# A feed-forward by pairs of tiles with seven products for eight, and weight sums made by the first tokens

## The chip, the cores and the metric

The kernel runs on one core of a Trainium2 chip. The metric is the time of one execution on the device, in microseconds (us); the time before is the median of three runs. Engines have short names: PE is TensorE's products, PEld its weight loads, DVE is VectorE, ACT is ScalarE, POOL is GpSimd, SP is the queue that issues all DMAs here.

## The reference

Two transformer layers over 32 sequences of 64 tokens, 512 wide, all in fp32. With `ln` for a layer norm:

```python
x = x + xattn0(ln(x), ctx)      # layer 0: one head, softmax over the 64 context rows
x = x + ffn0(ln(x))             # layer 0: a sparse feed-forward
x = x + xattn1(ln(x), ctx)      # layer 1: 32 query heads, 8 key/value heads of 128
x = x + ffn1(ln(x))             # layer 1: one dense product under two masks

def ffn0(xf):                               # 2048 tokens
    inter = xf @ c1_w.T @ c2_w.T            # rank 16, then 1792
    blk = inter.reshape(-1, 56, 32)
    idx = argmax(blk, -1) + arange(0, 1792, 32)   # the first of equals
    h = relu(einsum("bkm,bm->bk", w1[idx], xf))   # one of each 32 rows of w1
    return einsum("bk,bkm->bm", h, w2t[idx])
```

## The kernel before

The 2048 tokens are 16 tiles of 128 (`X[t]`), kept on chip throughout. Stages follow each other: attention of layer 0 by pairs of tiles, its feed-forward, attention of layer 1 in 32 units (four groups `T` of 512 tokens, eight groups `g` of heads), the last feed-forward. The kernel is written in program order against tiles taken from pools; a scheduler puts each engine's instructions in a fixed order at build time by simulated readiness, earlier code first, and adds the waits. On the chip each queue runs in that order. A pool that takes the bytes of released pools waits for all of their users.

**Feed-forward of layer 0.** `prep(t)` normalises a tile, turns it (`pt`, L181), copies it to `xT` and makes `z`, its 16 coefficients (`pz`, L404). `front(xT, z, half)` handles two quarters of 448 columns: `pi` (L414) is `z` against `C2`, sixteen rows deep; `ph` (L419) is `xT` against `W1` in four chunks, with all 1792 columns computed and the unchosen ones zeroed. The argmax is L421 (block maximum), L423 (equal to it), L426 on POOL (times 32..1, so that the first of equals wins), L427 (maximum), L428 (equal). L431 makes `g = max(ph, 0) * e`. `back(t, half, g)` turns `g` in seven pieces (`ptg`, L444), copies them to `gT` (L445) and multiplies by `W2` (`po`, L449); L454 adds to `x`. `finish` turns the first four tiles for layer 1.

**Large products of layer 1.** `winograd` makes a product of two by two quarters with seven products instead of eight. It needs four sums of the quarters on either side (`four_sums`, L99 to L107, on POOL) and adds into three banks of PSUM; `keep` takes a bank's value midway, `put` takes a finished quarter:

```python
mm(1, b1, True);  e1 = keep(0, b1)
mm(5, b2, True);  e5 = keep(1, b2)
mm(6, b1, False); u2 = keep(2, b1)
mm(2, b3, True);  put(0, 0, b3, e1)
mm(7, b1, False); put(1, 1, b1, e5)
mm(3, b2, False); put(0, 1, b2, u2)
mm(4, b1, False); put(1, 0, b1, None)
```

**Weight sums.** The sums of layer 1's weights (8 groups of `wq`, 8 of `wo`, 4 pairs of `wkv`) are made once, while layer 0 runs: `sum_weights` is called 8 times in the attention and 32 times in the feed-forward, and each call makes the sums of quarters `r` loaded by the call before (POOL), stores them to DRAM (L171, SP) and loads the next four (L176, SP). `load_weights` then loads, for each unit of layer 1, the quarters and sums that its seven products need (L505).

**A unit of layer 1** is `project_kv` (each second unit), `project_q`, `norms`, `keys`, `softmax` (L646, L653 to L663, three of its operations on POOL), `project_out` of the unit before (`wo`, L707), `attend` (`pta`, `pv` at L683) and `out_sums`.

Of the kernel before, what the change touches and what calls it, by code (L numbers as in the profile page):

```python
# [11 lines left out]
ALU = mybir.AluOpType  # L12
# [22 lines left out]
def tile_kernel(  # L35
# [39 lines left out]

    XG = [xpool.tile([P, 4, D], F32, name=f"x_{i}", tag=f"x_{i}") for i in range(4)]
# [19 lines left out]
    def four_sums(eng, s, w11, w12, w21, w22, right):  # L96

        if right:
            eng.tensor_tensor(s[0], w12, w11, ALU.subtract)  # L99
            eng.tensor_tensor(s[1], w22, s[0], ALU.subtract)  # L100
            eng.tensor_tensor(s[2], w22, w12, ALU.subtract)
            eng.tensor_tensor(s[3], w21, s[1], ALU.subtract)
        else:
            eng.tensor_tensor(s[0], w21, w22, ALU.add)
            eng.tensor_tensor(s[1], s[0], w11, ALU.subtract)  # L105
            eng.tensor_tensor(s[2], w11, w21, ALU.subtract)
            eng.tensor_tensor(s[3], w12, s[1], ALU.subtract)  # L107
# [3 lines left out]
    ORDER = (1, 5, 6, 2, 7, 3, 4)  # L111
    LEFT = {1: 0, 2: 1, 3: 7, 4: 3, 5: 4, 6: 5, 7: 6}
# [43 lines left out]
    to_sum = []  # L156
    for g in range(G):
        if g % 2 == 0:
            to_sum.append((kv_quarter, g // 2, WKS, True))
        to_sum.append((q_quarter, g, WQS, False))  # L160
        to_sum.append((o_quarter, g, WOS, True))
    loaded = []

    def sum_weights():

        if loaded:
            n, sums, right, r = loaded.pop()
            s = [wprep.tile([P, 2, 256], F32, name=f"s{k}", tag=f"s{k}") for k in range(4)]
            four_sums(nc.gpsimd, s, *r, right)
            for k in range(4):  # L170
                nc.sync.dma_start(sums[n][k], s[k])  # L171
        if to_sum:
            quarter, n, sums, right = to_sum.pop(0)
            r = [wprep.tile([P, 2, 256], F32, name=f"r{k}", tag=f"r{k}") for k in range(4)]
            for k in range(4):
                nc.sync.dma_start(r[k], quarter(n, k))  # L176
            loaded.append((n, sums, right, r))
# [6 lines left out]
    with ExitStack() as l0:  # L184
        w2pool = l0.enter_context(tc.tile_pool(name="ffnw", bufs=1, side="right"))
        C1 = w2pool.tile([P, C, RANK], F32, name="C1")
        C2 = w2pool.tile([RANK, INTER], F32, name="C2")
        W1 = w2pool.tile([P, C, INTER], F32, name="W1")
        W2 = w2pool.tile([P, 2 * HC, D], F32, name="W2")
        wprep = l0.enter_context(tc.tile_pool(name="wprep", bufs=1, side="right"))  # L190

        with ExitStack() as pa:
# [156 lines left out]
            for i in range(NP + 2):  # L349
# [3 lines left out]
                if i == 1:  # L353
                    nc.sync.dma_start(C1, c1)
                    nc.sync.dma_start(C2, c2)
                if 1 <= i < 5:
                    cs = slice((i - 1) * QW, i * QW)
                    nc.sync.dma_start(W1[:, :, cs], w1[:, :, cs])
                if i in (5, 6):
                    hs = slice((i - 5) * HC, (i - 4) * HC)  # L360
                    nc.sync.dma_start(W2[:, hs, :], w2[:, hs, :])
# [10 lines left out]
                if i >= 2:  # L372
                    sum_weights()


        tpool = ctx.enter_context(tc.tile_pool(name="tpool", bufs=2))
        XT0 = tpool.tile([P, C, 512], F32, name="xt_0", tag="xt")

        with ExitStack() as pb:
            wk = pb.enter_context(tc.tile_pool(name="ffnwork", bufs=2))  # L380
            ps_t = pb.enter_context(tc.tile_pool(name="ps_t1", bufs=2, space=PSUM))
            ps_i = pb.enter_context(tc.tile_pool(name="ps_i", bufs=2, space=PSUM))
            ps_h = pb.enter_context(tc.tile_pool(name="ps_h", bufs=2, space=PSUM))
            ps_o = pb.enter_context(tc.tile_pool(name="ps_o", bufs=1, space=PSUM))
            ps_z = pb.enter_context(tc.tile_pool(name="ps_z", bufs=1, space=PSUM))


            down = wk.tile([P, BLK], F32, name="down", bufs=1)
            nc.gpsimd.iota(
                down, pattern=[[-1, BLK]], base=BLK, channel_multiplier=0,  # L390
                allow_small_or_imprecise_dtypes=True,
            )
            down_b = down[:, None, :].to_broadcast([P, NBQ, BLK])

            def prep(t):
                xn = wk.tile([P, D], F32, name="xn2", tag="xn2")
                layernorm(xn, t)
                pt = ps_t.tile([P, C, P], F32, name="pt2", tag="pt")
                transposed(pt, xn)
                xT = wk.tile([P, C, P], F32, name="xT2", tag="xT2")  # L400
                nc.scalar.copy(xT, pt)
                pz = ps_z.tile([RANK, P], F32, name="pz", tag="pz")
                for c in range(C):
                    nc.tensor.matmul(pz, C1[:, c, :], xT[:, c, :], start=c == 0, stop=c == C - 1)  # L404
                z = wk.tile([RANK, P], F32, name="z", tag="z")
                nc.scalar.copy(z, pz)
                return xT, z

            def front(xT, z, half):
                g = wk.tile([P, 2 * QW], F32, name="g", tag="g")  # L410
                for q in range(2):
                    cs = slice((2 * half + q) * QW, (2 * half + q + 1) * QW)
                    pi = ps_i.tile([P, NBQ, BLK], F32, name="pi", tag="pi")
                    nc.tensor.matmul(  # L414
                        pi.rearrange("p a b -> p (a b)"), z, C2[:, cs], start=True, stop=True
                    )
                    ph = ps_h.tile([P, QW], F32, name="ph", tag="ph")
                    for c in range(C):
                        nc.tensor.matmul(ph, xT[:, c, :], W1[:, c, cs], start=c == 0, stop=c == C - 1)  # L419
                    m = small.tile([P, 2, NBQ], F32, name="m", tag="m")  # L420
                    nc.vector.tensor_reduce(m[:, 0, :], pi, AX.X, ALU.max)  # L421
                    e = wk.tile([P, NBQ, BLK], F32, name="e", tag="e", bufs=3)
                    nc.vector.tensor_tensor(  # L423
                        e, pi, m[:, 0, :, None].to_broadcast([P, NBQ, BLK]), ALU.is_equal
                    )
                    nc.gpsimd.tensor_tensor(e, e, down_b, ALU.mult)  # L426
                    nc.vector.tensor_reduce(m[:, 1, :], e, AX.X, ALU.max)  # L427
                    nc.vector.tensor_tensor(  # L428
                        e, e, m[:, 1, :, None].to_broadcast([P, NBQ, BLK]), ALU.is_equal
                    )  # L430
                    nc.vector.scalar_tensor_tensor(  # L431
                        g[:, q * QW : (q + 1) * QW], ph, 0.0,
                        e.rearrange("p a b -> p (a b)"), ALU.max, ALU.mult,
                    )
                return g

            po = {}

            def back(t, half, g):
                gT = wk.tile([P, HC, P], F32, name="gT", tag="gT", bufs=1)  # L440
                for a, n in ((0, 4), (4, HC - 4)):
                    pt = ps_t.tile([P, n, P], F32, name="ptg", tag="pt")
                    for k in range(n):
                        nc.tensor.transpose(pt[:, k, :], g[:, (a + k) * P : (a + k + 1) * P], ident)  # L444
                    nc.scalar.copy(gT[:, a : a + n, :], pt)  # L445
                if half == 0:
                    po[t] = ps_o.tile([P, D], F32, name="po2", tag="po")
                for k in range(HC):
                    nc.tensor.matmul(  # L449
                        po[t], gT[:, k, :], W2[:, half * HC + k, :],  # L450
                        start=half == 0 and k == 0, stop=half == 1 and k == HC - 1,
                    )
                if half == 1:
                    nc.vector.tensor_add(X[t], X[t], po.pop(t))  # L454

            def finish(t):
                xn = wk.tile([P, D], F32, name="xn3", tag="xn2")
                layernorm(xn, t)
                pt = ps_t.tile([P, C, P], F32, name="pt3", tag="pt")
                transposed(pt, xn)  # L460
                nc.scalar.copy(XT0[:, :, t * P : (t + 1) * P], pt)

            ready = prep(0)
            pend = None
            for t in range(NT):
                xT, z = ready
                for half in range(2):
                    if half == 1 and t + 1 < NT:
                        ready = prep(t + 1)
                    g = front(xT, z, half)  # L470
                    sum_weights()
                    if pend is not None:
                        back(*pend)
                        if pend[1] == 1 and pend[0] < 4:
                            finish(pend[0])
                    pend = (t, half, g)
            back(*pend)
# [3 lines left out]
    with ExitStack() as pc:  # L481
        wst = pc.enter_context(tc.tile_pool(name="l1w", bufs=1))
# [406 lines left out]
```

## Time and profile before

| | us |
|---|---|
| median of three runs | 2166.94 (2165.83 to 2170.69) |
| the profiled execution, its own time | 2171.68 |
| its span, first to last instruction | 2169.7 |
| PE busy in the span | 2048.7 |
| DVE, ACT, POOL busy | 933.2, 601.7, 602.9 |
| feed-forward of layer 0, first to last product | 204.9 to 751.4 |
| first product of layer 1 | 756.5 |

In rows of instruction groups and timelines, `out<-in` gives the tiles written and read, then the partitions by elements, and `xN` the number of instructions. An fp32 product appears as two MATMUL instructions. The shown duration of one MATMUL includes its way through the array, so the spacing of starts is what a stream of them costs. A bracket such as `[1.24 <-POOL e]` is idle time of that engine before the instruction, and what ended it.

### The profile page before, as it was taken

How to read it: one execution, taken by the hardware profiler on the slowest of the kernel's cores; microseconds unless marked ns; L12 is line 12 of the kernel's file. 1: busy time of each engine (PE TensorE's matmuls, PEld its weight loads, DVE VectorE, ACT ScalarE, POOL GpSimd, SP SyncE). 2: the span in 40 equal slices, each digit the busy share in tenths (PEclk: the TensorE clock that was granted, in tenths of full speed). 3: DMA queues.
4: the chain of work that ended last, by engine and by line, in shares of the span. 5: the costliest groups of instructions: out<-in, count | busy, mean ns of one | idle time of the engine just before them, and what ended most of it. 6: DMA issues, size and time to landing. Idle time of an engine off the chain costs nothing.

```text
span 2169.7 us, 24349 instructions
## 1 busy us (share of the span) xinstructions
PE 2048.7 (94%) x9300; PEld 1442.9 (67%) x9300; DVE 933.2 (43%) x1712; ACT 601.7 (28%) x1077; POOL 602.9 (28%) x512
## 2 busy tenths in 40 slices
PE   8898499999999899999999999999999999999994
PEld 4454244444444478888888888888888888888752
DVE  5554254544444334334444334344344344344446
ACT  3442010110000043343333333333333333333220
POOL 1345621211111022323422324423324322322302
PEclk9998799999999999999999999999999999999997
DMA  8866600000000053344343344334334334333102
GB/s 288 282 224 199 207 20 0 1 1 0 0 1 0 30 175 114 115 117 134 108 118 113 115 113 139 110 112 120 113 113 136 112 107 122 117 107 93 56 8 77
DMA packets 152994, 223.29 MB, mean 103 GB/s; under 512 B 13024, under 2 KB 84832, under 8 KB 151984
## 3 DMA queue, kind: packets, MB, share of 16 engines
q1 hardware_dynamic: 152880, 221.75, 33.2%
q8 instruction: 74, 1.21, 0.2%
q14 instruction: 40, 0.33, 0.0%
HBM read 196.53 MB, written 25.17 MB: 102 GB/s over the span
## 4 chain that ended last, share of the span: by engine, by line
PE 75%; POOL 9%; DVE 7%; DMA 4%; ACT 2%; issue 2%; SPq 1%; POOLq 0%; DVEq 0%; ACTq 0%
PE b L516 36%; PE po L449 9%; PE ph L419 8%; PE sc L646 4%; PE pv L683 3%; POOL prob L654 3%; PE pd L794 3%; PE pi L414 2%; POOL prob L657 2%; PE pq L269 2%; DVE mx L656 2%; PE pr L609 2%; DMA r<-in_wq 1%; PE pta L673 1%; PE pk L254 1%
## 5 line engine op out<-in xcount | busy, mean ns | idle before, releaser
L516 PE MATMUL b<-wo,so 128*128 128x256 f32 x1024 | 244.6, 381 | 0.7 <-POOL so L105 0.5
L516 PE MATMUL b<-tx,wq 128*128 128x256 f32 x1024 | 241.5, 381 | 1.8 <-ACT keep L523 1.8
L419 PE MATMUL ph<-W,xT 128*128 128x448 f32 x512 | 213.2, 554 | 28.5 <-DVE g L431 28.5
L707 DVE TENSOR_TENSOR x<-x,b 128x512 f32<-128x512 f32 x224 | 150.3, 678 | 199.7 <-PE b L516 199.5
L654 POOL TENSOR_TENSOR prob<-prob,msk 128x512 f32<-128x512 f32 x64 | 81.6, 1275 | 554.9 <-DVE prob L653 498.0
L516 PEld LDWEIGHTS b<-tx,wq 128*128 128x128 f32 x1024 | 192.9, 190 | 33.0 <-issue 5.0
L516 PE MATMUL b<-wo,oT 128*128 128x256 f32 x768 | 195.4, 388 | 15.7 <-DVE x L707 15.4
L516 PEld LDWEIGHTS b<-wo,so 128*128 128x128 f32 x1024 | 189.3, 190 | 24.4 <-POOL so L105 0.9
L449 PE MATMUL po<-W,gT 128*128 128x512 f32 x448 | 200.8, 600 | 3.2 <-ACT gT L445 3.2
L516 PE MATMUL b<-xt,wq 128*128 128x256 f32 x768 | 185.7, 381 | 0.0
L516 PEld LDWEIGHTS b<-wo,oT 128*128 128x128 f32 x768 | 139.6, 190 | 65.8 <-issue 26.3
L426 POOL TENSOR_TENSOR e<-e,down 128x448 f32<-128x448 f32 x64 | 72.5, 1133 | 381.4 <-DVE e L423 381.4
L419 PEld LDWEIGHTS ph<-W,xT 128*128 128x128 f32 x512 | 93.2, 192 | 126.9 <-issue 80.1
L516 PEld LDWEIGHTS b<-xt,wq 128*128 128x128 f32 x768 | 143.4, 190 | 24.0 <-issue 5.8
L449 PEld LDWEIGHTS po<-W,gT 128*128 128x128 f32 x448 | 82.5, 190 | 115.1 <-issue 91.6
L591 DVE TENSOR_TENSOR qT<-b,keep 128x512 f32<-128x512 f32 x96 | 66.4, 692 | 164.8 <-PE b L516 164.8
L646 PEld LDWEIGHTS sc<-kT,qT 128*128 128x128 f32 x1024 | 123.0, 192 | 6.9 <-DVE prob L653 4.5
L445 ACT COPY gT<-ptg 128x512 f32<-128x512 f32 x64 | 30.9, 535 | 338.7 <-PE ptg L444 338.7
L646 PE MATMUL sc<-kT,qT 128*128 128x64 f32 x1024 | 123.0, 273 | 0.0
L516 PE MATMUL b<-wkv,sc 128*128 128x256 f32 x512 | 119.6, 383 | 0.0
L593 ACT ACTIVATE qsq<-qT 128x512 f32<-128x512 f32 x128 | 80.6, 630 | 127.7 <-DVE qT L591 126.7
L660 ACT ACTIVATE prob<-prob 128x512 f32<-128x512 f32 x64 | 40.3, 630 | 272.3 <-POOL prob L657 272.3
(177 smaller groups left out, 2856.7 us busy)
## 6 DMA issues: line engine op xcount, KB each, us to landing
wq<-wqs SPq DMA_DIRECT2D x128, 256.0 KB, 2.6
wo<-wos SPq DMA_DIRECT2D x128, 256.0 KB, 2.7
wq<-in_wq SPq DMA_DIRECT2D x96, 256.0 KB, 2.9
wo<-in_wo SPq DMA_DIRECT2D x96, 256.0 KB, 2.9
wkv<-wks SPq DMA_DIRECT2D x64, 256.0 KB, 2.6
wkv<-in_wkv SPq DMA_DIRECT2D x48, 256.0 KB, 2.7
r<-in_wq SPq DMA_DIRECT2D x32, 256.0 KB, 4.3
wqs<-s SPq DMA_DIRECT2D x32, 256.0 KB, 2.1
```

The lines of the kernel that those rows point to most:

```text
L269: nc.tensor.matmul(pq, xT[:, tt, c, :], WQ[:, c, :], start=c == 0, stop=c == C - 1)
L419: nc.tensor.matmul(ph, xT[:, c, :], W1[:, c, cs], start=c == 0, stop=c == C - 1)
L426: nc.gpsimd.tensor_tensor(e, e, down_b, ALU.mult)
L449: nc.tensor.matmul(po[t], gT[:, k, :], W2[:, half * HC + k, :], start=half == 0 and k == 0, stop=half == 1 and k == HC - 1,)
L516: nc.tensor.matmul(out[:, h, :], lhs(h, c), rhs(h, c), start=first and h == 0 and c == 0, stop=c == 1, skip_group_check=True,)
L591: nc.vector.tensor_add(o, ps, kept.rearrange("p j (b t) -> p j b t", t=S))
L593: nc.scalar.activation(qsq[:, 4 * th : 4 * th + 4, 2 * hh : 2 * hh + 2, :], o, AF.Square)
L646: nc.tensor.matmul(sc[:, 4 * a + 2 * pp + b, :], qT[:, bb, 2 * pp : 2 * pp + 2, :].rearrange("p h t -> p (h t)"), kT[:, bb * S : (bb + 1) ...
L654: nc.gpsimd.tensor_tensor(pr, pr, msk_b, ALU.add)
L683: nc.tensor.matmul(pv[:, b, a, :], kv[rows, 2 * h + a, HD : 2 * HD], aT[rows, a, :], start=True, stop=True,)
L707: nc.vector.tensor_add(xq[:, i, j], xq[:, i, j], ps)
L794: nc.tensor.matmul(pd, xT[:, c, :], WD[:, c, :], start=c == 0, stop=c == C - 1)
```

## The change

The feed-forward of layer 0 works on pairs of tiles. Both of its large products, `xT` by `W1` and `g` by `W2`, go through `winograd`: the first as two tiles by two quarters of 448 columns for each half `u` of the columns, the second as two tiles by two halves of 256 columns. The sums of `W1` are made on POOL during the attention and those of `W2` after the first front, those of `xT` in `prep`, those of `gT` in `back`. One of the four quarters of each operand is used by no product itself and is overwritten by a sum (`UNUSED`).

For the argmax, `C1R` repeats the 16 columns of `C1` at columns 0, 32, 64 and 96, so `z` holds the coefficients four times, at four groups of rows; `C2R` holds each quarter of `C2` at one of them. The two `pi` of a half are issued next to each other on different row groups.

`sum_weights` goes. In layer 1 the first group of tokens (`T == 0`) loads the four quarters of each weight, makes the sums on POOL in place, uses them and stores them; the other tokens load as before. `finish` goes, and `tokens(0)` turns the first tiles. The pools of the feed-forward and of layer 1 have `reuse_waits="tile"`: a tile waits only for the users of earlier tiles on its own bytes.

```diff
     ORDER = (1, 5, 6, 2, 7, 3, 4)
+    UNUSED = {False: 2, True: 1}
...
-    def sum_weights():
...
+        W1 = [[place(f"w1_{u}_{k}") for k in range(4)] for u in range(2)]
+        for u in range(2):
+            s = [place(f"w1s_{u}_{k}") for k in range(3)]
+            W1[u] += [s[0], s[1], W1[u][UNUSED[True]], s[2]]
...
                 if i == 1:
                     nc.sync.dma_start(C1, c1)
-                    nc.sync.dma_start(C2, c2)
+                    for q in range(4):
+                        nc.gpsimd.tensor_copy(C1R[:, :, q, 0:RANK], C1)
+                        nc.sync.dma_start(C2R[32 * q : 32 * q + RANK, :], c2[:, q * QW : (q + 1) * QW])
                 if 1 <= i < 5:
...
+                    u, kk = (i - 1) // 2, (i - 1) % 2
+                    for n in range(2):
+                        nc.sync.dma_start(
+                            W1[u][2 * kk + n],
+                            w1[:, 2 * kk : 2 * kk + 2, (2 * u + n) * QW : (2 * u + n + 1) * QW],
+                        )
+                if i in (4, 6):
+                    w = W1[(i - 4) // 2]
+                    four_sums(nc.gpsimd, w[4:], *w[:4], True)
...
-                if i >= 2:
-                    sum_weights()
...
+            ps_p = pb.enter_context(tc.tile_pool(name="ps_p", bufs=4, space=PSUM, reuse_waits="tile"))
+            ps_t = pb.enter_context(tc.tile_pool(name="ps_t1", bufs=2, space=PSUM, reuse_waits="tile"))
+            ps_i = pb.enter_context(tc.tile_pool(name="ps_i", bufs=2, space=PSUM, reuse_waits="tile"))
...
+            def chosen(z, m, u):
+                es = []
+                for n in range(2):
+                    q = 2 * u + n
+                    rows = slice(32 * q, 32 * q + RANK)
+                    pi = ps_i.tile([P, NBQ, BLK], F32, name="pi", tag="pi")
+                    nc.tensor.matmul(
+                        pi.rearrange("p a b -> p (a b)"), z[rows, m * P : (m + 1) * P], C2R[rows, :],
+                        start=True, stop=True,
+                    )
+                    es.append(pi)
+                for n in range(2):
...
+            def front(xq, z, u):
+                e = [chosen(z, m, u) for m in range(2)]
+                g = [gpool.tile([P, 2, QW], F32, name="g", tag="g", bufs=3) for m in range(2)]
...
+                def keep(n, ps):
+                    h = wk.tile([P, QW], F32, name=f"hk{n}", tag="hk", bufs=3)
+                    nc.scalar.copy(h, ps)
+                    return h
+                def put(m, n, ps, kept):
+                    if kept is not None:
+                        nc.vector.tensor_add(kept, ps, kept)
+                        ps = kept
+                    nc.vector.scalar_tensor_tensor(g[m][:, n, :], ps, 0.0, e[m][n], ALU.max, ALU.mult)
+                winograd(lambda: ps_p.tile([P, QW], F32, name="ph", tag="pp"), mm, keep, put)
...
+            def back(p, gq):
+                s = [gpool.tile([P, HC, P], F32, name=f"gs{k}", tag=f"gs{k}") for k in range(3)]
+                q = gq + [s[0], s[1], gq[UNUSED[False]], s[2]]
+                four_sums(nc.gpsimd, q[4:], *gq, False)
...
+            for p in range(NT // 2):
+                xq, z = ready
+                g = front(xq, z, 0)
+                if last is not None:
+                    turn(last[1], last[0], 1)
+                    back(p - 1, last[0])
+                else:
+                    four_sums(nc.gpsimd, W2[4:], *W2[:4], True)
+                gq = [None] * 4
+                turn(g, gq, 0)
+                g = front(xq, z, 1)
+                if p + 1 < NT // 2:
+                    ready = prep(p + 1)
+                last = (gq, g)
+            turn(last[1], last[0], 1)
+            back(NT // 2 - 1, last[0])
...
+        def load_weights(w_in, sums, n, T, right, tag, bufs):
+            use = RIGHT if right else LEFT
...
+            by = {use[i]: w for i, w in out.items()}
+            by[UNUSED[right]] = by[6]
+            if T == 0:
+                for k in (1, 0, 3, 2) if right else (2, 3, 0, 1):
+                    nc.sync.dma_start(by[k], w_in(n, k))
+                four_sums(nc.gpsimd, [by[k] for k in range(4, 8)], *(by[k] for k in range(4)), right)
+                for k in range(4):
+                    nc.sync.dma_start(sums[n][k], by[4 + k])
+            else:
+                for i in ORDER:
+                    k = use[i]
+                    nc.sync.dma_start(out[i], w_in(n, k) if k < 4 else sums[n][k - 4])
```

## The prediction

> **What bounds the kernel now.** I read the page first, then the busy times by stretch, TensorE's waits, the timelines of one token tile and of two places where small products share the array.
>
> ```profile
> PE 2048.7 (94%) x9300; PEld 1442.9 (67%) x9300; DVE 933.2 (43%) x1712; ACT 601.7 (28%) x1077; POOL 602.9 (28%) x512
> ```
>
> TensorE is the only engine near its span. The stretches (length, then the busy time of PE, PEld, DVE, ACT, POOL, then granted clock, DMA share, GB/s) show where that holds.
>
> ```profile
> 204.80:220.00 15.20, 14.08 (x46) 6.72 (x46) 2.63 (x3) 1.68 (x4) 8.67 (x7) 0.88 0.62 210
> 220.00:247.00 27.00, 0.00 (x0) 0.00 (x0) 2.07 (x3) 0.00 (x0) 17.35 (x15) 0.54 0.70 232
> ...
> 408.80:663.00 254.20, 254.20 (x754) 119.33 (x753) 116.61 (x201) 24.56 (x56) 36.15 (x32) 1.00 0.00 0
> ...
> 751.60:771.00 19.40, 14.54 (x57) 12.42 (x57) 5.33 (x15) 2.24 (x5) 0.00 (x0) 0.82 0.85 281
> ```
>
> The feed-forward of layer 0 runs from 204.9 to 751.4 us. Through most of it TensorE is never idle, so each microsecond of products removed there is a microsecond of time. Its beginning is a hole of 27 us, and its end another of 5. TensorE's waits in this stage name the first; the timeline shows who held it.
>
> ```profile
> PE ph L419 <- DVE g L431: 28.5, 1, 28.5
> ```
>
> ```profile
> 242.52 1.26 POOL L107 TENSOR_TENSOR sc<-ct,sc 128x512 f32<-128x512 f32 x1
> 243.74 1.13 POOL L426 TENSOR_TENSOR e<-e,down 128x448 f32<-128x448 f32 x1
> 244.82 1.26 POOL L99 TENSOR_TENSOR s<-r,r 128x512 f32<-128x512 f32 x1
> 244.90 0.62 DVE L427 TENSOR_REDUCE m<-e 128x14 f32<-128x448 f32 x1 [32.87 <-POOL e L426]
> ```
>
> DVE waited 32.87 us for one multiplication of 1.13 us on POOL. It stood in POOL's queue behind the weight sums (L99 to L107), and these waited for their loads: the chain of that stretch goes DMA r, POOL s, SPq L171, SPq L176, DMA r, about 10 us a round.
>
> Now one tile of the steady state on TensorE; the difference of two starts is the cost of a group.
>
> ```profile
> 413.10 1.05 PE L404 MATMUL pz<-xT,C 128*16 128x128 f32 x8
> 414.08 2.52 PE L419 MATMUL ph<-W,xT 128*128 128x448 f32 x6
> 416.53 1.01 PE L414 MATMUL pi<-C,z 16*128 16x448 f32 x2
> 417.47 3.27 PE L419 MATMUL ph<-W,xT 128*128 128x448 f32 x8
> 420.58 0.93 PE L444 MATMUL ptg<-ident,g 128*128 128x128 f32 x7
> 421.44 1.01 PE L414 MATMUL pi<-C,z 16*128 16x448 f32 x2
> 422.38 6.28 PE L449 MATMUL po<-W,gT 128*128 128x512 f32 x14
> 428.50 3.17 PE L419 MATMUL ph<-W,xT 128*128 128x448 f32 x8
> ```
>
> Each fp32 product is two instructions. 448 columns take 0.376 us each (3.10 / 8, less 0.1 for the change of kind), 512 columns 0.429, a pi of 16 rows 0.94 for its two. The same group returns after 31.75 us: ph 12.62, po 12.24, pi 3.76, ptg 1.72, pz 0.98, pt 0.43. A pair of tiles is 63.5.
>
> **What the Trainium skill says.** TensorE: Matmul & The Clock Gate, Part 3 (Packing small matmuls): products on different row groups of the array run concurrently. The trace agrees on groups of 64 rows: eight instructions of 256 columns take 1.07 us (802.72 to 803.79), where eight on the full array take 1.73.
>
> ```profile
> 771.00 1.89 PE L516 MATMUL b<-xt,wq 128*128 128x256 f32 x8
> 772.73 3.62 PE L516 MATMUL b<-tx,wq 128*128 128x256 f32 x16
> ```
>
> ```profile
> 802.72 1.14 PE L683 MATMUL pv<-aT,kv 64*128 64x256 f32 x8
> 803.79 1.99 PE L516 MATMUL b<-tx,wq 128*128 128x256 f32 x8
> ```
>
> That is four slots of 0.216 and 0.2 for the change. Groups of 32 rows are not in the trace. The same page, Part 1 (architectural detail), says that the queues of DVE, ACT and GPSIMD are strict FIFO; the 32.87 us above are that. Its Part 1 also says that an idle array falls to half clock; here 0.54 in the hole, and the eight ph after it took 5.66 us instead of 3.1. SBUF — State Buffer, Who interferes with whom: a DVE instruction with two SBUF inputs contends with a GpSimd one that reads SBUF; here L428 took 1.02 beside L99 and 0.62 otherwise.
>
> **The steady state, for each pair.** ph: seven products of two chunks, twice, is 56 instructions x 0.376 + 0.6 for changes = 21.7; before 25.2. po: seven of seven chunks at 256 columns is 98 x 0.216 + 0.3 = 21.5; before 24.5 (two of 256 columns cost 0.432 where one of 512 costs 0.429, so nearly the whole eighth is kept). pz: 8 x 0.216 + 0.1 = 1.8, before 2.0. ptg and pt stay, 4.3. pi is the unknown. The two of a u, back to back, cost 2 x 0.376 + 0.2 = 0.95 instead of 1.88. But they own only two banks (ps_i), which DVE frees one at a time, so the second token tile's pair is likely to be issued apart. All paired: 3.8; half: 5.7; none: 7.5, as before. I take half. More switching between interleaved groups: 1.0, ten times 0.1. Sum 56.0, bounds 53 and 58 — 7.5 us less a pair.
>
> What hides the rest: DVE has eight argmaxes of 4 x 0.655 (start to start) = 21, eight L431 forms 5.2, six additions of kept banks 3.9, seven half additions to x at about 0.42 = 3 and two layernorms 3.3: 36 of 56. ACT gains six copies of 0.55; it was at 10% in this stage. POOL has eight e at 1.13, four x sums of 256 elements (half of 1.27) and four g sums of 896 (1.75 x 1.27 = 2.2): 20.5. All fit, but the margin inside a front is small. The last of its seven products adds into a bank that DVE must have read, and DVE has 10.5 of argmax before that, plus two puts: about 13 to 14 us after the first pi, when TensorE is through the other six at 12. The 2 us are filled by the transposes of g and by the fourth bank of ps_p. In the back, product five needs the first g sum: copy 0.5 and sum 2.2 beside product one, 3.0. I leave 1 us a pair for misses (0 to 4). Eight pairs: 8 x 6.5 = **52 us** gained.
>
> **The beginning.** The 80 loads and 80 stores of 256 KB and the 80 sums of layer 0 go; so POOL's and SP's queues no longer hold e. Gained: 28.5, 2.6 of half clock, and about 4 of smaller waits. New there: W1's eight sums of 896 elements (18 us) beside the attention, where POOL has nothing else; W2's four of 1792 (4.5 each), behind a load of 896 KB of the kind that now takes 9.4 us, in POOL's queue with the first e; and three fronts without a back between them, where DVE's 16 us exceed TensorE's 14.5. W1 comes in eight loads instead of four and C2 in four instead of one, the same bytes, and C1R takes a memset and four small copies: nothing, under 150 us of attention; were one late, the first front would wait for it. I charge 10 for the rest (5 to 20) and take back 3, since waits by tile let the first pair start inside the attention's tail (7.5 of each 10 us busy between 190 and 210). Net **+28**.
>
> **Into layer 1.** Now 5.1 us idle and 1.8 at low clock, because wkv's loads wait for the pool below. After, these bytes are W1's, free before the last back (22 us), so loads and tokens(0) fall under it. But POOL has then 9 of g sums, 5 each of tx, sc, wkv and wq: 29 us for a shadow of 23. wq is needed 12 us later; I keep 3 us of wait. Net **+4** (-3 to +7). The 16 transposes of finish only change place.
>
> **Layer 1, first tokens.** The 80 sums, 102 us at 1.27, are now spread over eight units of 41 us. POOL goes from 13.6 us a unit to 26. SP has 80 loads and 80 stores where it had 140 loads; a store waits for POOL, and the loads behind it wait too. POOL's softmax operations (L654, L657, L663) then stand behind a sum, or behind a sum that waits for its load (2.7 us). What covers this is project_out, 12 us of products beside a softmax of 8 to 9. The trace has no such unit: nothing at best, 1.5 us a unit at worst, no gain since TensorE loses only 1.4% there. I take **-4** (0 to -12). Later tokens: unchanged.
>
> **Sum.** 52 + 28 + 4 - 4 = 80 us off a profiled 2171.68 (span 2169.7): 2092. The median of the runs shown is 4.7 lower, 2166.94, so **2087**.
>
> **Rivals.** (1) The fronts lock on DVE, half hidden: 4 us a pair and 10 more at the beginning, 2087 + 24 + 10, about 2120. For it: e's round over POOL, 1.24 us idle on DVE at every quarter now. Against: with two pi side by side DVE has the other quarter to do in that time. (2) Row groups do not overlap or never meet: pi stays 7.5, 15 us lost, 2102. (3) Slower: DVE goes quarter by quarter as now, 3.86 us each; four are 15.4, with two puts 18, against TensorE's 12. That is 6 us at each of 16 fronts, 99 us, if nothing fills it; 99 against 80 is about 2186. It decides from 5 us a front on. Against: transposes, prep and one spare bank hold 4.5 of it, and DVE was only 46% busy. (4) POOL starves layer 1's first tokens: 12 and 3 at the entry, about 2105. (5) All goes well: pi paired, no misses, nothing lost later, 2052.
>
> **Numbers.** Forecast 0.64, (1) 0.12, (2) 0.08, (3) 0.05, (4) 0.06, (5) 0.05. All but (3) are faster; a mix of (1) and (4) may land near zero. 0.2% (4 us, what a measurement of this kernel can tell from no change) gives faster 0.93, same 0.02, slower 0.05. The range 2046 to 2136 holds the forecast's bounds, (1), (2), (4) and most of (5).
>
> **What would show it.** Right: ph in 448 instructions (8 x 56; 512 before), the back's in 784 of 256 columns; a pair returning every 55 to 58 us; no wait above 10 us at the feed-forward's start; no DMA r. pi whose two products start together show (2) wrong. DVE waits of TensorE above 2 us at each front show (1) or (3). Waits of sc, b or pta for POOL before the second tokens show (4). A pair above 61 us, or a hole over 20 us at either end of the feed-forward, would make the forecast wrong.

## The result, and the profile after

The kernel after takes 2130.98 us (median of 4 runs, 2130.47 to 2134.59), the kernel before beside it 2168.05. The ratio is 0.9832, interval 0.9815 to 0.9849: about 37 us less. The profiled execution took 2131.04 us (span 2129.2), 40.6 less than that of before. The forecast was 80 us less, 2087. The sign was right, the size about half.

The busy times of the page of after, then the stretches of the feed-forward and the entry into layer 1 (columns as in the prediction):

```profile
PE 1997.6 (94%) x9508; PEld 1496.2 (70%) x9508; DVE 956.3 (45%) x1801; ACT 624.6 (29%) x1117; POOL 735.9 (35%) x592
```

```profile
203.70:251.80 48.10, 38.16 (x103) 18.20 (x102) 34.78 (x59) 7.52 (x17) 28.17 (x17) 0.82 0.08 24
251.80:311.50 59.70, 57.73 (x215) 36.68 (x214) 31.57 (x62) 8.96 (x21) 21.94 (x17) 0.97 0.00 0
...
691.20:705.40 14.20, 2.95 (x17) 1.97 (x16) 10.53 (x28) 3.69 (x10) 10.53 (x8) 0.63 0.58 197
705.40:736.80 31.40, 31.34 (x144) 26.35 (x145) 7.02 (x12) 9.85 (x17) 15.01 (x12) 0.95 0.44 142
```

TensorE's busy time fell by 51 us, the span by 40. The first two stretches run from one pair's pz to the next pair's; the last two run from the end of the last po (691.2) to the first product of layer 1 (705.4) and on to its first scores (736.8). A pair of tiles comes back after 59.7 us, not 57. The hole of 27 us at the beginning is gone, but the first pair, which has no back, takes 48.1. Between the feed-forward and layer 1 lies a new hole of 14.2 us at clock 0.63.

When starts of the same work in the two traces are set side by side, their difference is the lead of the kernel after over the kernel before:

| mark | before | after | lead, us |
|---|---|---|---|
| first pz | 207.3 | 203.7 | 3.6 |
| last po ends | 751.5 | 691.2 | 60.3 |
| first product of layer 1 | 756.5 | 705.4 | 51.1 |
| first scores | 788.7 | 736.8 | 51.9 |
| scores from the second tokens on | | | 39.3, constant |

So 60 us were won by the end of the feed-forward, and 21 of them lost by the end of layer 1's first tokens. TensorE's waits (total, times, longest) name three of the places: the first pair, the other pairs, and layer 1 up to the second tokens.

```profile
PE ptg L481 <- DVE g L470: 7.7, 1, 7.7
```

```profile
PE ph L456 <- DVE hk L468: 11.3, 11, 1.2
PE pi L428 <- DVE e L438: 3.6, 7, 0.5
PE po L493 <- POOL gs L112: 2.7, 8, 0.3
```

```profile
PE pta L732 <- POOL prob L722: 8.7, 6, 1.6
PE b L578 <- DMA ct<-in_cT: 8.5, 1, 8.5
```

The steady pair on TensorE, and then DVE in its front of `u` = 0:

```profile
373.71 1.02 PE L428 MATMUL pi<-C2R,z 16*128 16x448 f32 x4
374.66 1.02 PE L456 MATMUL ph<-w1s,xs 128*128 128x448 f32 x2
376.19 0.98 PE L428 MATMUL pi<-C2R,z 16*128 16x448 f32 x2 [0.51 <-DVE e L438]
...
427.18 1.77 PE L456 MATMUL ph<-w1s,xT 128*128 128x448 f32 x4 [0.93 <-DVE hk L468]
```

```profile
377.28 0.62 DVE L442 TENSOR_REDUCE m<-e 128x14 f32<-128x448 f32 x1 [0.71 <-POOL e L441]
...
379.99 0.62 DVE L442 TENSOR_REDUCE m<-e 128x14 f32<-128x448 f32 x1 [0.49 <-POOL e L441]
...
382.69 0.62 DVE L442 TENSOR_REDUCE m<-e 128x14 f32<-128x448 f32 x1 [0.49 <-POOL e L441]
...
385.40 0.62 DVE L442 TENSOR_REDUCE m<-e 128x14 f32<-128x448 f32 x1 [0.49 <-POOL e L441]
```

Two pi on two row groups start together: their four instructions take 0.95 us (373.71 to 374.66), the time of one pi alone. But DVE comes round once per quarter in 2.70 us and starts the last instruction of a front 14.9 us after its first maximum (374.8 to 389.7), while TensorE needs about 12 by the prediction's sum.

A part of that round is new. POOL's multiplication of e took 1.13 us in the kernel before, and it takes that here only at a front's first quarter:

```profile
414.84 1.13 POOL L441 TENSOR_TENSOR e<-e,down 128x448 f32<-128x448 f32 x1 [15.33 <-DVE e L438]
417.23 1.44 POOL L441 TENSOR_TENSOR e<-e,down 128x448 f32<-128x448 f32 x1 [1.26 <-DVE e L438]
```

```profile
417.07 0.62 DVE L443 TENSOR_TENSOR e<-e,m 128x448 f32<-128x448 f32 x1
```

From the second pair on, 42 of the 56 multiplications overlap a DVE L443 and take about 1.44 us; the other 14 overlap none and take 1.13. DVE's next maximum waits for the multiplication, so I estimate 0.3 us more in each such round.

### The profile page after: what moved, and what is told of

Its sections match the earlier page's. It is cut to its first block, busy times and chain, and to the rows that moved or that the text cites. A ratio compares the mean times of both kernels' runs of the same rounds, so it can differ in the third digit from the quotient of the medians.

```text
span 2129.2 us, 24834 instructions
## 1 busy us (share of the span) xinstructions
PE 1997.6 (94%) x9508; PEld 1496.2 (70%) x9508; DVE 956.3 (45%) x1801; ACT 624.6 (29%) x1117; POOL 735.9 (35%) x592
## 4 chain that ended last, share of the span: by engine, by line
PE 72%; DVE 11%; POOL 11%; issue 3%; ACT 3%; DMA 1%; SPq 0%; POOLq 0%; ACTq 0%; DVEq 0%
PE b L578 38%; PE po L493 7%; PE sc L705 4%; PE pv L742 3%; POOL e L441 3%; PE ph L456 3%; POOL prob L713 3%; PE pd L853 2%; PE pq L266 2%; POOL prob L716 2%; PE pr L668 2%; PE pk L251 2%; DVE m L442 1%; DVE e L438 1%; DVE mx L715 1%
## 5 line engine op out<-in xcount | busy, mean ns | idle before, releaser
L578 PE MATMUL b<-wo,oT 128*128 128x256 f32 x768 | 195.4, 388 | 15.8 <-DVE x L766 15.4
L441 POOL TENSOR_TENSOR e<-e,down 128x448 f32<-128x448 f32 x64 | 85.6, 1340 | 190.3 <-DVE e L438 190.3
L585 ACT COPY keep<-b 128x512 f32<-128x512 f32 x144 | 84.2, 585 | 84.7 <-PE b L578 84.6
L578 PEld LDWEIGHTS b<-wkv,sc 128*128 128x128 f32 x512 | 96.1, 190 | 16.8 <-issue 4.0
L578 PE MATMUL b<-wkv,ct 128*128 128x256 f32 x384 | 97.9, 391 | 8.5 <-DMA ct<-in_cT 8.5
L748 DVE COPY oT<-pv 128x512 f32<-128x512 f32 x64 | 44.1, 690 | 132.8 <-PE pv L742 132.8
L112 POOL TENSOR_TENSOR so<-oT 128x512 f32<-128x512 f32 x32 | 40.5, 1266 | 177.4 <-ACT oT L748 177.4
```

The costliest lines, as they stand in the source:

```text
L578: nc.tensor.matmul(out[:, h, :], lhs(h, c), rhs(h, c), start=first and h == 0 and c == 0, stop=c == 1, skip_group_check=True,)
L585: nc.scalar.copy(e, ps)
L748: eng(o, pv[:, b].rearrange("p a (j t) -> p a j t", t=S))
```

## The experiments

Every kernel below was timed against the kernel before in the same way. What is "gained" is against the 2130.98 us of after; the intervals are about 4 us wide on either side. Where a few us decide, they are read from the same marks as in the table of leads, in the one profiled execution of each kernel.

### Layer 1's part alone

The kernel before without `sum_weights`, and with `load_weights` of the kernel after.

> The kernel before with one part of the change alone: layer 1's weight sums are made by its first tokens, the feed-forward is left as it was. The raw loads, sums and stores of the first half go. Theory (the traces of before and after): the 28.5 us hole ahead of the feed-forward and its half clock go (-31), and the first tokens of layer 1 take 12.6 us more, as they do in the kernel after: 2168 - 31 + 12.6 = about 2150 us, the first layer-1 product 31 us earlier and the lead down by 12 to 13 at the end of the first tokens. The prediction's sizes: the first tokens lose 4 us, so 2141. Rival: the hole has another cause than the raw loads and stays: 2165 or more.

Measured: 2145.83 us, ratio 0.9907 (0.9886 to 0.9929). The first pz comes at 191.1, and the last po ends at 704.9, a lead of 46.6. The beginning that held the 27 us hole is now this:

```profile
191.10:240.80 49.70, 49.70 (x146) 22.84 (x146) 26.42 (x48) 5.76 (x12) 14.22 (x12) 1.00 0.03 11
```

The removal was worth more than the 35 us of the hole and its neighbours, because the attention ahead of it (16 us) was held back by the same loads, sums and stores. The entry into layer 1 then loses 8.6 us (lead 46.6 to 38.0), with TensorE waiting 5.6 us for a load of wkv and 5.6 for one of wq, and 13.8 us are lost from the first scores to the second tokens: this part brings both costs with it, whatever the feed-forward is.

### First tokens without sums

```diff
-            if T == 0:
-...
+            for i in ORDER:
+                nc.sync.dma_start(out[i], w_in(n, use[i] % 4))
```

All tokens take raw quarters here, so layer 1's weight sums are left out, and with them their stores.

> The kernel after, but the first tokens of layer 1 (and all others) load raw quarters in place of the sums: seven loads, no sums on POOL, no stores. It leaves out layer 1's weight sums. Theory: the 12.6 us that the first tokens lose are POOL's sums, behind which the softmax's POOL instructions wait, and the stores in SP's queue ahead of ct's load are part of the 14.3 us hole at the entry: 2131 - 12.6 - (3 to 8) = 2110 to 2116 us, the wait of pta for POOL prob gone. Rival: the loss comes from layer 1's pools now standing on other addresses, whatever is loaded: no change, 2128 to 2133.

Measured: 2116.54 us, 0.9764 (0.9747 to 0.9781). The lead is 55.2 at the first scores and 55.2 at the end: the loss of 12.6 is gone. The hole falls from 14.2 to 3.9, but the sums of the context (sc) then keep TensorE waiting for 5.3.

### First tokens' sums on DVE

```diff
-four_sums(nc.gpsimd, [by[k] for k in range(4, 8)], ...)
+four_sums(nc.vector, [by[k] for k in range(4, 8)], ...)
```

> The kernel after with the weight sums of layer 1's first tokens made by DVE in place of POOL. Theory: the softmax's three POOL instructions stood behind the sums in POOL's queue; on DVE a sum is shorter and the queue less full, so most of the 12.6 us comes back: the first tokens lose 2 to 5 us, 2121 to 2124 us, the wait of pta for POOL prob is gone. Rival: the sums stand in a queue ahead of the softmax either way, and DVE has six instructions of each softmax: the loss stays at 12 or grows, 2130 to 2138.

Measured: 2118.61 us, 0.9781 (0.9761 to 0.9800), 12 gained. The wait of the first tokens is down from 8.7, and 2.4 us of lead are lost instead of 12.6:

```profile
PE pta L732 <- POOL prob L722: 2.1, 4, 0.6
```

The loads and stores are the same, and the sums cost a fifth. So what cost time was the sums in POOL's queue, ahead of the softmax's three instructions. A sum is also shorter on DVE (medians 0.68 us for wkv and 0.91 for wo, against 1.27 on POOL), and no run tells the two apart.

### The argmax without its tie-break

```diff
-nc.gpsimd.tensor_tensor(e, e, down_b, ALU.mult)
-nc.vector.tensor_reduce(mx[:, 1, :], e, AX.X, ALU.max)
-nc.vector.tensor_tensor(e, e, mx[:, 1, :, None].to_broadcast(...), ALU.is_equal)
```

> The kernel after without the tie-break of the argmax (e is the first equality; POOL's multiply, DVE's second maximum and DVE's second equality are left out). Theory: the steady pair of 59.6 us is paced in its fronts by the DVE and POOL round of 2.70 us a quarter; with the round near 1.3 us the waits (1.05 ph to pi, 1.1 and 1.2 at the fronts' last products, part of pi's) go: 56 to 57 us a pair, 8 x 3 = 24 us, and the beginning, where these instructions stood behind the W2 sums, gains 5 more: about 2103 us. Rival: the 2.6 us that a pair takes above the working are TensorE's own switches and half clock: pair 59 to 60, total 2125 to 2131.

Measured: 2120.92 us, 0.9787 (0.9770 to 0.9804), 10 gained. Two pairs:

```profile
366.70:424.10 57.40, 56.04 (x216) 36.10 (x215) 23.81 (x46) 8.97 (x20) 11.03 (x9) 1.00 0.00 1
424.10:482.90 58.80, 57.71 (x216) 36.77 (x215) 23.84 (x46) 8.99 (x21) 11.05 (x9) 0.97 0.00 0
```

57.4 at full clock is the forecast's 57. Every second pair loses 1.4 more to an episode of half clock of about 3.4 us at the pi. In the kernel after these alternate too, but both sorts take 59.7: what the clock spares, the wait for DVE takes. So my theory was half right: of the 2.7 us above the forecast's 57 about 1.7 is the round over DVE and POOL, on the mean, and 0.8 the clock.

### The second argmax moved into the back

```diff
 g = front(xq, [chosen(z, m, 0) for m in range(2)], 0)
...
-back(p - 1, last[0])
+back(p - 1, last[0], [lambda: ahead(0), lambda: ahead(1)])   # one after each product
```

`ahead(m)` runs `chosen(z, m, 1)`; e has eight buffers, xn2 one.

> The kernel after with the argmax of the second half of a pair issued between the products of the back before it, where DVE is idle for 22 us (eight buffers of e, one of xn2). The work is the same. Theory: the fronts are paced by DVE's round; taking half of it out of them gives what leaving out the tie-break gave (1.7 us a pair) and, if the half-clock episode at pi goes too, 0.8 more: a pair of 57 to 58 us, 2112 to 2119 us. Rival: it is each front by itself that is paced, so the front of u=0 keeps its waits and only half comes back: 58.8, about 2124; and pi between po products costs switches: 59.5, 2130.

Measured: 2168.09 us, 0.9995 (0.9987 to 1.0004). The whole gain is lost; a pair takes 64.9. Neither the theory nor its rival had foreseen the reason, which the timeline of the back shows:

```profile
405.01 1.02 PE L428 MATMUL pi<-C2R,z 16*128 16x448 f32 x4
405.96 3.29 PE L493 MATMUL po<-w2s,gs 128*128 128x256 f32 x14
409.18 1.01 PE L428 MATMUL pi<-C2R,z 16*128 16x448 f32 x2
413.79 1.83 PE L428 MATMUL pi<-C2R,z 16*128 16x448 f32 x2 [3.60 <-DVE e L438]
```

The second two pi come 4 us after the first two. They need the two banks back, and DVE takes 5.4 for two quarters. The rest of the back stands behind them in TensorE's queue, so TensorE is idle for 3.60 us in the middle of the back, and the clock is lower (0.92 over the pair). The same move with the pi after the second and the fifth product:

> As the kernel with the argmax in the back, but its pi pairs stand after the second and the fifth of the back's seven products in place of after the first and the second. There a pair took 64.9 us, because the second pi pair stood 3.1 us behind the first while DVE needs 5.4 us for two quarters, and TensorE waited 4 to 5 us a pair in the middle of the back and lost its clock. Theory: with 9 us between the pi pairs DVE is ready in time and the fronts of u=1 are no longer paced: 57 to 58.5 us a pair, 2112 to 2122 us. Rival: pi between po products trips the half clock wherever it stands, or xn2's single buffer is what costs: 61 us or more, 2140 or more.

Measured: 2121.52 us, 0.9778 (0.9761 to 0.9796), 9.5 gained. Pairs are 58.2 at full clock, all alike:

```profile
369.90:428.10 58.20, 55.06 (x215) 35.18 (x214) 31.92 (x62) 9.18 (x19) 21.62 (x16) 1.00 0.00 1
```

DVE has the same 31.9 us of work in the pair as in the kernel after. Its place changed and not its amount, so pacing and not load was the matter. A part of the gain is in pi: six of a pair's eight now start two at a time, as at 373.71 above, where only two did, and pi falls from 6.4 to 4.7 us a pair. The edit's other change, eight buffers of e and one of xn2, was not run alone; none of DVE's waits in the steady pairs of the kernel after is for a buffer of e.

### The sums of W2 and of W1

First without W2's sums (the call left out, raw quarters in their place):

> The kernel after without the sums of W2 (their products take raw quarters; the sums of W2 are left out). Theory: in the beginning the e multiplications wait on POOL behind the four sums of 4 us and DVE's second equality takes 3.31 us beside them; without them the first front falls from 31 to 14 to 18 us: 12 to 17 us less, 2114 to 2119 us. Rival: the first front is late because the argmax starts cold, sums or not: 0 to 5 us less, 2126 to 2131.

Measured: 2125.46 us, 0.9804 (0.9790 to 0.9819), 5.5 gained, not my theory's 12. The first pair falls by 10.7; in this execution 1.6 of that goes to a later first pz and 1.5 to the first tokens. The range of 12 to 17 took the whole first front for the sums' doing. What the sums did beside DVE is in the timelines of the kernel after, POOL and then DVE:

```profile
211.32 3.96 POOL L108 TENSOR_TENSOR w2s<-w,w2s 128x1792 f32<-128x1792 f32 x1
215.24 1.52 POOL L441 TENSOR_TENSOR e<-e,down 128x448 f32<-128x448 f32 x1
```

```profile
212.46 3.31 DVE L443 TENSOR_TENSOR e<-e,m 128x448 f32<-128x448 f32 x1
```

The Trainium skill, SBUF — State Buffer, Who interferes with whom, says that a DVE instruction with two SBUF inputs contends with a GpSimd one that reads SBUF. The trace agrees: 3.31 us where 0.61 is usual, and it ends 0.5 us after POOL's sum. Beside that, e's multiplication stands behind the sums in POOL's queue. The next kernel makes the sums on DVE; the scheduler puts one of them ahead of the first argmax, one inside it and two after the second front:

```diff
-else:
-    four_sums(nc.gpsimd, W2[4:], *W2[:4], True)
...
 g = front(xq, z, 1)
+if p == 0:
+    four_sums(nc.vector, W2[4:], *W2[:4], True)
```

> The kernel after with the sums of W2 on DVE, two of them ahead of the first argmax and two after the second front (1.9 us each by the size, where POOL took 4.0). Without them at all the first pair took 37.4 us in place of 48.1. Theory: half of that comes back, since DVE is still delayed by the two at the start: the first pair 41 to 44 us, 2124 to 2127 us. Rival: DVE paces the first front by itself, so that its own sums cost as much as POOL's: 46 to 48, 2129 to 2131.

Measured: 2123.88 us, 0.9789 (0.9772 to 0.9807), 7 gained, slightly more than without the sums, though the two intervals overlap. The first two sums take 2.00 and 2.40 us, where POOL took 3.96 for each. The first pair falls from 48.1 to 34.9 us, but the second grows from 59.7 to 63.1, with the last two sums at 240.5 and 243.5 us, next to its first argmax. W1's sums in the same way, in the attention:

> The kernel after with the sums of W1 (in layer 0's attention) made by DVE in place of POOL. In the kernel before with the sums of layer 1 alone moved, the first pz came at 191.1 us; in the kernel after at 203.7. Theory: those 12.6 us are the eight POOL sums between 33.6 and 59.2 us, beside which DVE's instructions are late and psc waits 5.8 us: on DVE they take about 1 us each in a queue half idle, and pz comes at 193 to 196: 2121 to 2124 us. Rival: it is the loads of W1 as eight pieces, which delay ct and cn in SP's queue and stay: pz at 202 to 204, 2129 to 2132.

Measured: 2123.84 us, 0.9803 (0.9788 to 0.9819), 7 gained; the first pz is at 195.4. A sum takes 1.07 us instead of 2.1 to 2.5, and this wait of the kernel after (33 to 75 us) is gone:

```profile
PE psc L290 <- DVE s L293: 5.8, 1, 5.8
```

What came before it on DVE, first in the kernel after beside two of POOL's sums, then with the sums on DVE:

```profile
50.00 2.25 POOL L107 TENSOR_TENSOR w1s<-w,w 128x896 f32<-128x896 f32 x1
52.33 2.13 POOL L108 TENSOR_TENSOR w1s<-w,w1s 128x896 f32<-128x896 f32 x1
```

```profile
50.25 4.50 DVE L93 TENSOR_SCALAR xn<-x,mv,rs 128x512 f32<-128x512 f32 x2
```

```profile
47.88 1.00 DVE L93 TENSOR_SCALAR xn<-x,mv,rs 128x512 f32<-128x512 f32 x2
```

So POOL's sums held up DVE here too, 4.50 us for two instructions in place of 1.00, and these read one large tile and not two.

### The entry into layer 1

The queue of SP in the kernel after shows what stands ahead of the load of the context (ct):

```profile
663.36 1.29 SPq L561 DMA_DIRECT2D wkv<-in_wkv  x3
...
683.59 4.12 SPq L564 DMA_DIRECT2D wqs<-wq  x4
687.77 1.99 SPq L561 DMA_DIRECT2D wo<-in_wo  x4
693.98 4.69 SPq L564 DMA_DIRECT2D wos<-wo  x4
...
700.02 0.54 SPq L604 DMA_DIRECT2D ct<-in_cT  x1
```

Stores that wait for POOL's sums stand between wkv's loads and ct's. The pool that holds ct reached into g's pool, which is used to the end of the last back. The edit keeps it over the work buffers alone:

```diff
 cpool = pc.enter_context(tc.tile_pool(name="l1ctx", bufs=1, reuse_waits="tile"))
+spool = pc.enter_context(tc.tile_pool(name="l1sum", bufs=1, reuse_waits="tile"))
...
-s = [cpool.tile(... name=f"tx_{T}_{k}" ...   (sc_ the same)
+s = [spool.tile(... name=f"tx_{T}_{k}" ...
```

> The kernel after with layer 1's sums of tokens and contexts in a pool of their own, so that ct, xt and xn1 lie over the work buffers of the feed-forward alone and not over g, gT and gs: ct's load then stands second in SP's queue of layer 1 in place of behind the stores of wks, wqs and wos. Theory: the hole of 14.3 us between the last po and the first product is ct's place in that queue: 4 to 6 us are left, 2121 to 2124 us. Rival: the weight sums on POOL are the next late ones: the time from the first product to the first scores grows from 31.4 to 37 or more, as it did with raw weights, and 3 us are gained, 2128.

Measured: 2130.08 us, 0.9831 (0.9812 to 0.9850): no change that can be told. ct's load is issued at 673.17 and the hole is 0.7 us, but the first scores take 40.1 us after the first product instead of 31.4. The rival was right in its mechanism. POOL shows why:

```profile
700.88 1.26 POOL L107 TENSOR_TENSOR wo<-wo,wo 128x512 f32<-128x512 f32 x1 [4.23 <-DMA wo<-in_wo]
...
705.87 1.26 POOL L112 TENSOR_TENSOR sc<-ct 128x512 f32<-128x512 f32 x1
```

POOL idles for wo's load, makes sums that are wanted later, and only then sc's, for which TensorE stands 7.5 us. The entry gains 4.8 us, and the second pair happened to lose 3.7 here (63.4, at clock 0.92): the clock falls in its front of `u` = 1, where eight ph take 6.1 us, start to start, and 3.1 in the kernel after. What set that off is not settled. With the first tokens' sums on DVE, sc in the early pool and xt in the other:

> The kernel after with both parts of the entry mended: ct, sc and xn1 in a pool over the feed-forward's work buffers alone (so that ct's load and sc's sums stand ahead in SP's and POOL's queues) and the weight sums of the first tokens on DVE. With ct early alone the wait moved to sc's sums behind wo's on POOL (7.5 us); with DVE sums alone sc waited 5.6 us for the late ct. Theory: with both, the time from the last po to the first scores falls from 45.6 us to 33 to 36 and the first tokens lose 2 to 3: 2131 - 10 - 10 = 2108 to 2112 us. Rival: the sums of wkv and wq on DVE, behind its last instructions of the feed-forward, are the next late ones: 41 us stay, 2117 to 2119, as with DVE sums alone.

Measured: 2111.02 us, 0.9736 (0.9714 to 0.9758), 20 gained. Last po to first scores: 35.5 us instead of 45.6, where DVE's sums alone leave 41.6 and the early context alone 40.8. Either alone leaves the other queue's wait for sc (5.6 and 7.5 us); with both it is gone.

### All together

W1's, W2's and the first tokens' sums on DVE and the entry's pool split; then with the spaced argmax; then with the argmax of the next pair's first half in the front before it as well (`prep` ahead of that front, the sums of x after it).

> The kernel after with W1's sums, W2's sums (two early, two after the second front) and the first tokens' weight sums on DVE, and the entry's pool split. If the parts add up: 7.5 (W1) + 5 (W2) + 20 (entry and first tokens) less than the kernel after, 2097 to 2100 us. Rival: they share DVE at the start of the feed-forward and the first pair grows again: 2102 to 2106.

Measured: 2093.84 us, 0.9648 (0.9623 to 0.9673), 37 less than after.

> All the parts that gained, in one kernel: W1's, W2's and the first tokens' sums on DVE, the entry's pool split, and the second half's argmax between the back's products. If the prediction's 80 us failed in these places and nowhere else, they add up: 37 us (three together) and 10 (the spaced argmax) less than the kernel after, 2083 to 2086 us, a steady pair of 58.2. Rival: the places share DVE, and some of the 47 us is counted twice: 2088 to 2094.

Measured: 2085.76 us, 0.9623 (0.9601 to 0.9644), 45 less than after. Taken singly the four edits gave 7.1 (W1), 7.1 (W2), 9.5 (argmax) and 20.0 (entry and first tokens), 43.7 in sum. Within the intervals they add up, so the places are separate.

> As all parts together, with the argmax of the next pair's first half issued in the front before it as well (its norm and pz go ahead of that front). Theory: what is left of DVE's pacing is the front of u=0 (the waits of 1.05 and 1.47 us in each pair): a pair of 56.5 to 57.5, 8 to 12 us less than all parts, about 2075. Rival: the two argmaxes now meet in the front of u=1, DVE is late there instead, and the next front waits for its sums of x at once: 58 to 60, no gain or a loss of up to 10, 2084 to 2094.

Measured: 2079.83 us, 0.9593 (0.9575 to 0.9611), the fastest kernel here. Pairs:

```profile
399.50:456.90 57.40, 54.78 (x216) 35.13 (x215) 32.48 (x63) 9.00 (x19) 21.65 (x16) 1.00 0.00 0
456.90:515.90 59.00, 56.39 (x216) 35.66 (x215) 32.58 (x62) 9.00 (x19) 21.65 (x16) 0.97 0.00 1
```

57.4 again at full clock, as without the tie-break, and the half-clock episode is back in one of the three pairs from 399.5 us on (the third takes 57.3). The total gains 6 on the kernel before it, with intervals that overlap, and less than the 8 to 12 expected.

## Why the prediction was half right

| step | forecast | measured | from |
|---|---|---|---|
| steady pairs | 52 | 30 | 8 x (63.5 - 59.7) |
| beginning | 28 | 30 | lead of 60.3 at the last po, less 30 |
| entry into layer 1 | +4 | -8.4 | lead 60.3 to 51.9 |
| first tokens | -4 | -12.6 | lead 51.9 to 39.3 |
| sum | 80 | 39 | |

**Steady pairs.** The mechanism held: eighths of both products, pi in row groups, nothing on DMA. Start to start over two pairs of after, each pair has ph 24.5, po 22.5, pi 6.4, ptg 3.3, pz 1.7, pt 1.3. Against the forecast, ph is 2.8 too long, po 1.0 and pi 0.7: the forecast took half of a pair's eight pi as starting two at a time, and only the first two do. The step that failed is "I leave 1 us a pair for misses": its place (the last product of a front behind DVE) was named, its size was 3.7 over the 56. DVE needed 14.9 us from its first maximum (16 from the first pi), where the text had 13 to 14 from the first pi, and the transposes and the spare bank did not fill the rest. A term that the text left out is the contention within the argmax itself: it priced POOL's multiplication at 1.13 us, and three of four take 1.44. By my estimate of 0.3 us a round that is about 0.9 us of a front; no run separates it. This is rival (1), the fronts locked on DVE, at 2.7 us a pair above the forecast in place of its 4, a part of which is the clock (0.8). The sign that the text gave for it, a wait above 2 us at each front, did not come in the steady pairs; the longest is 1.2. The text saw DVE's busy share and not that DVE is idle in the back, where it could have worked ahead; spacing the argmax shows that.

**Beginning.** Right in sum by two errors. Taking away the loads and sums was worth 46.6 and not 35, for the attention gained too. The new work cost about 16 (46.6 + 30 - 60.3) and not 7: W1's sums, said to lie where "POOL has nothing else", held up DVE's instructions, and W2's did the same to the first argmax. Moving the two gave 7 each. The text cited the contention of DVE and POOL and then counted only POOL's queue. Of the 16 us, 12.6 lie ahead of the first pz (191.1 us with layer 1's part alone, 203.7 in the kernel after). Moving W1's sums brings it to 195.4, and the 4.3 left are not accounted for.

**Entry.** The step that failed is "loads and tokens(0) fall under it". wkv's and wq's loads did (from 663 us); ct's did not: it stood in SP's queue behind stores that the change itself adds. The text counted POOL's 29 us against the shadow of 23, which was the right worry for the second queue, and never placed ct's load in the first.

**First tokens.** The term was 4 with 12 as its bound; it is 12.6. Its mechanism, the softmax behind the sums in POOL's queue, is shown by the kernels with raw weights (0 lost) and with DVE's sums (2.4 lost). Rival (4) had it (its two terms add up to 2102, not 2105).

The forecast's 2087 is about what the four repairs together measure, 2085.76. It priced a kernel in which its own warnings cost little. What stays open is what sets off the half clock, in the second pair with the context early above all, and the 4.3 us of the attention.

## What to carry to other kernels

Before work is charged at nothing because "the engine is idle there", ask what stands behind it in that engine's queue, which instructions of the other engine it lengthens, and which stores wait for it in the queue of loads. A share of busy time says nothing about pacing: an engine at half load that is idle in one stage and needed in step in the next sets the time, and work issued ahead must be spaced by that engine's round, not by the products. When one wait at an entry is cleared, look for the next queue before calling it done.

## What was new in the hardware

- Products of 16 rows on row groups of 32 run two at a time: 0.95 us for the four instructions of two products, where the two of one product take 0.94 alone.
- One POOL sum of 1792 elements stretched a DVE instruction with two SBUF inputs from 0.61 to 3.31 us, and DVE's L442, a maximum over one input, stayed at 0.62 beside it. A single large input is no safeguard: beside sums of 896 elements xn (TENSOR_SCALAR) went from 0.50 to 2.25 us each. It works the other way too: POOL's multiplication took 1.44 us beside DVE's L443, and 1.13 otherwise.
- On DVE itself the sums of 896 take 1.07 us, on POOL 2.1 to 2.5 in the attention.
- Half-clock episodes came with waits of up to about 1 us at the pi (0.97 over a pair) and not only with long holes; they cost 1.4 to 1.6 us where TensorE bounds the pair (57.4 against 58.8, 57.4 against 59.0) and almost nothing in the kernel after, where DVE does (59.6 against 59.8).
